# A graph network on one core: the count stretch's one-hot keys, four chunks in one two-tensor operation

## The chip, the core and the metric

The kernel runs on one core of one Trainium2 chip. The metric is device time in microseconds from the first to the last instruction of one execution, median of several runs; lower is better. The engines are named as in the profile: PE (matrix products) with PEld (its weight loads), DVE (the vector engine), ACT (the scalar engine), POOL (GpSimd, which here also issues the indirect gathers) and SP (which issues most other DMAs).

## What is computed

A stack of four graph networks over 3125 nodes with 128 features and 100,000 edges, sorted by destination, each with a residual connection. Cut to its core:

```python
edge_index = jnp.stack([src, dst])
h = jnp.maximum(_layernorm(x, axis=-1), 0.0)
x = x + _L0_gnn_ref(h, ...)   # 3 attention layers, softmax over each node's incoming edges
h = jnp.maximum(_layernorm(x, axis=-1), 0.0)
x = x + _L1_gnn_ref(h, ...)   # messages: an MLP on (h[src], h[dst], edge_attr), mean per node
h = jnp.maximum(_layernorm(x, axis=-1), 0.0)
x = x + _L2_gnn_ref(h, ...)   # 2 attention layers with 4 heads
h = jnp.maximum(_layernorm(x, axis=-1), 0.0)
x = x + _L3_gnn_ref(h, ...)   # 2 convolutions with normalized edge weights
```

In the first of these networks an edge's attention weight depends on its source and its destination node alone, so parallel edges weigh the same. What the kernel needs is therefore the number of edges from each node to each node:

```python
e = leaky_relu((h @ a_src[l])[src] + (h @ a_dst[l])[dst], 0.2)
p = exp(e - m[dst]);  s = segment_sum(p, dst);  alpha = p / s[dst]
z = segment_sum(alpha[:, None] * h[src], dst) + b[l]
```

## The kernel before

Nodes stand in NT = 25 tiles of P = 128. Edges are sorted by destination, so the edges of a small range of destinations are a run in memory. A *window* is NW = 16 destinations; there are 196. Its edges are loaded from a start that is found at run time, as k chunks of 128 edges (one edge per partition), with k fixed ahead from the distribution (`Plan`, `plan.cw`): edges that belong to a neighbour window are masked. An edge is packed in one integer `code`. The windows come in four batches, each decoded at once:

- batch 1, 8 windows of 59, 25, 20, 17, 15, 13, 12 and 12 chunks
- batch 2, 32 windows: 8 each of 11, 8, 7 and 6 chunks
- batch 3, 64 windows: 8 of 6, 24 of 5 and 32 of 4 chunks
- batch 4, 92 windows: 24 of 4 and 68 of 3 chunks

That is 1025 chunks in all. The stages follow each other: preparation and count (`count_edges`, up to 440 us), the three attention layers (to about 1070), the messages (to about 2190), the two attention layers with four heads (`dynamic_attention_layer`, to about 4560) and the two convolutions.

**The count stretch.** The count of edges from source node s to destination d is a product of one-hot matrices. For each chunk, `by_src` (128 edges x 128) marks the low seven bits of the edge's source, and `by_key` (128 edges x n_key = 400) marks its key, that is the source's tile (25) times 16 plus the destination's place in the window. PE multiplies `by_src` (the stationary operand) by `by_key` (the moving one) and adds the chunks of a window up in one PSUM bank; banks A, B and C take turns. Then ACT copies the bank to `count` as bytes (L1096), and runs a ReLU with a sum over it (L1099), which flags counts over 255. `by_src` is made for up to eight chunks by one two-tensor comparison in the helper `even` (L1040, recorded as L1043): the row of low bits is broadcast, the chunks are the innermost dimension, and an odd number of chunks is rounded up. `by_key` is made chunk by chunk by a comparison of the constant row `iota_key` with one number per partition (L1092), into six buffers.

Before each batch, `code` (one buffer) is loaded by one DMA per window on SP's queue (L1058), decoded by DVE (L1071 to L1080) and copied to `keep` by ACT (L1081); `keep` is stored (L1082) for later. The next batch's loads can start when `code` has been decoded. The tile framework reorders instructions on each engine, so the layer norm at the start (L866 to L877) and the decoding are interleaved with the products.

**The layers with four heads.** Edges come in 30 larger windows (`plan.ew`) of 59, 43, 30 ... 18 and 8 chunks, in groups of C = 4 chunks: 220 groups in a layer. For each group POOL issues four gathers into one buffer `g2` of a pool of G2 = 20 (`gather`, L1348), PE adds its transposes to the other term (L1376), DVE and ACT make the scores; a window later the group's message is made from the same buffer (L1847), which frees it, and summed by PE (L1852). The constant G2 also decides how far apart a window's scoring and its sums are issued: where the steps (groups) of windows i - 1, i and i + 1 add up to less than G2, the sums of window i - 1 are left for the next round (`apart`). For windows 15 to 20 these sums are 21, 20, 19, 18, 18 and 18.

Beside these layers the generator `adjacency` builds the weighted adjacency of the convolutions with one-hot products of its own (L1771, L1775), a step at a time; each of the 196 windows ends with a copy to `rows` on ACT (L1781; two buffers, as the pool has) and a store on SP's queue (L1782).

Of the kernel before, what the change touches and what calls it, by code (L numbers as in the profile page):

```python
# [8 lines left out]
F32 = mybir.dt.float32  # L9
BF16 = mybir.dt.bfloat16  # L10
I32 = mybir.dt.int32
AF = mybir.ActivationFunctionType
ALU = mybir.AluOpType
# [5 lines left out]
P = 128  # L19
C = 4  # L20
# [673 lines left out]
F16 = mybir.dt.float16  # L694
U8 = mybir.dt.uint8
SP = mybir.EngineType.SP
NW = 16
# [47 lines left out]
def sorted_path(ctx: ExitStack, tc: tile.TileContext, a: dict, out: bass.AP, flag_out: bass.AP):  # L745

    nc = tc.nc
# [21 lines left out]
    def bc(ap, shape):  # L769
        return ap.to_broadcast(shape)  # L770
# [32 lines left out]
                   allow_small_or_imprecise_dtypes=True)  # L803
    iota_by = const.tile([P, P, 8], BF16, name="iota_by")
    nc.vector.tensor_copy(iota_by, bc(iota_row[:, :, None], [P, P, 8]))
    weights = []

    def load_matrix(name, src):
# [231 lines left out]
    def even(out_t, a_t, row, j0, n, op):  # L1040

        n += n % 2
        nc.vector.tensor_tensor(out_t[:, :, :n], a_t[:, :, :n], bc(row[:, None, j0:j0 + n], [P, P, n]), op)  # L1043

    def count_edges(count):

        with tc.tile_pool(name="f_cw", bufs=2) as wp:
            tail0 = plan.nw * NW
            nc.vector.memset(count[:, :, tail0:], 0)
            many = wp.tile([P, plan.nw], F32, name="many", bufs=1)  # L1050
            below_255 = wp.tile([P, 1], F32, name="below_255", bufs=1)
            nc.vector.memset(below_255, -254.0)
            for w0, w1, c0, cols in plan.batches:
                code = wp.tile([P, cols, 2], I32, name="code", bufs=1)
                own = wp.tile([P, cols], F32, name="own", bufs=1)
                for w, col, k in plan.cw[w0:w1]:
                    r = at_register(base_c, w, P * k)
                    reads.append(nc.sync.dma_start(  # L1058
                        code[:, col - c0:col - c0 + k, :],
                        codes[bass.ds(r, P * k), :].rearrange("(p k) i -> p k i", p=P)))  # L1060
                    nc.gpsimd.memset(own[:, col - c0:col - c0 + k + k % 2], float(w))
                    if k % 2:
                        nc.gpsimd.memset(code[:, col - c0 + k:col - c0 + k + 1, :], 0)
                ti = wp.tile([P, cols], I32, name="ti", bufs=1)
                tf = wp.tile([P, cols], F32, name="tf", bufs=1)
                keep = wp.tile([P, 3, cols], F32, name="keep", bufs=2)
                key = keep[:, 0, :]
                low = wp.tile([P, cols], BF16, name="low", bufs=2)
                code_i = code[:, :, 0]

                nc.vector.tensor_scalar(ti, code_i, 16, None, ALU.logical_shift_right)  # L1071
                nc.vector.tensor_tensor(own, ti, own, ALU.not_equal)
                nc.vector.tensor_scalar(ti, code_i, 127, None, ALU.bitwise_and)
                nc.vector.scalar_tensor_tensor(keep[:, 1, :], own, FAR, ti, ALU.mult, ALU.add)
                nc.vector.tensor_copy(low, keep[:, 1, :])

                nc.vector.tensor_scalar(ti, code_i, 12, NW - 1, ALU.logical_shift_right, ALU.bitwise_and)
                nc.vector.tensor_copy(tf, ti)
                nc.vector.tensor_scalar(ti, code_i, 7, 31, ALU.logical_shift_right, ALU.bitwise_and)
                nc.vector.scalar_tensor_tensor(key, ti, float(NW), tf, ALU.mult, ALU.add)  # L1080
                nc.scalar.copy(keep[:, 2, :], code[:, :, 1].bitcast(F32))  # L1081
                nc.sync.dma_start(kept[:, :, c0:c0 + cols], keep)  # L1082
                for w, col, k in plan.cw[w0:w1]:
                    pt = bank("ABC"[w % 3])
                    for k0 in range(0, k, 8):
                        kn = min(8, k - k0)
                        j0 = col - c0 + k0
                        by_src = wp.tile([P, P, 8], BF16, name="by_src", bufs=3)
                        even(by_src, iota_by, low, j0, kn, ALU.is_equal)
                        for i in range(kn):  # L1090
                            by_key = wp.tile([P, n_key], BF16, name="by_key", bufs=6)
                            nc.vector.tensor_scalar(by_key, iota_key, key[:, j0 + i:j0 + i + 1], None,  # L1092
                                                    ALU.is_equal)
                            nc.tensor.matmul(pt[:, :n_key], by_src[:, :, i], by_key,  # L1094
                                             start=(k0 + i == 0), stop=(k0 + i == k - 1))
                    nc.scalar.copy(count[:, :, w * NW:(w + 1) * NW],  # L1096
                                   pt[:, :n_key].rearrange("p (t d) -> p t d", d=NW))
                    junk = wp.tile([P, n_key], BF16, name="junk")
                    nc.scalar.activation(junk, pt[:, :n_key], AF.Relu, bias=below_255,  # L1099
                                         accum_out=many[:, w:w + 1])  # L1100
            worst = wp.tile([P, 1], F32, name="worst", bufs=1)
            nc.vector.tensor_reduce(worst, many, AX.X, ALU.add)
            pt = bank("D")
            nc.tensor.matmul(pt[:1, :1], worst, ones[:, 0:1], start=True, stop=True)
            nc.vector.tensor_copy(flags[:, 3:4], pt[:1, :1])
            load_edge_windows(wp)
            for t in range(NT):
                own_t = count[:, t, t * P:(t + 1) * P]
                nc.vector.tensor_add(own_t, own_t, ident)
# [630 lines left out]
    def adjacency(pool):  # L1740
        for t in range(NT):
            ws = [c for c in plan.cw if c[0] // per == t]
            c0, cols = ws[0][1], ws[-1][1] + ws[-1][2] + ws[-1][2] % 2 - ws[0][1]
            pk = pool.tile([P, 3, cols], F32, name="pk", padded_shape=[P, 3, most_cols])
            nc.sync.dma_start(pk, kept[:, :, c0:c0 + cols])
            low = pool.tile([P, cols], BF16, name="low", padded_shape=[P, most_cols])
            w1 = pool.tile([P, cols], BF16, name="w1", padded_shape=[P, most_cols])
            w2 = pool.tile([P, cols], BF16, name="w2", padded_shape=[P, most_cols])
            w3 = pool.tile([P, cols], BF16, name="w3", padded_shape=[P, most_cols])
            yield  # L1750
            nc.scalar.copy(low, pk[:, 1, :])
            nc.scalar.copy(w1, pk[:, 2, :])
            nc.vector.tensor_sub(pk[:, 2, :], pk[:, 2, :], w1)
            nc.scalar.copy(w2, pk[:, 2, :])
            nc.vector.tensor_sub(pk[:, 2, :], pk[:, 2, :], w2)
            nc.scalar.copy(w3, pk[:, 2, :])
            yield
            for w, col, k in ws:
                sums = bank("W")
                for k0 in range(0, k, C):  # L1760
                    kn = min(C, k - k0)
                    j0 = col - c0 + k0
                    by_src = pool.tile([P, P, C], BF16, name="by_src")
                    even(by_src, iota_by, low, j0, kn, ALU.is_equal)
                    by_wgt = [pool.tile([P, P, C], BF16, name=f"by_wgt{q}") for q in range(3)]
                    for q, part in enumerate((w1, w2, w3)):
                        even(by_wgt[q], by_src, part, j0, kn, ALU.mult)
                    yield
                    by_key = pool.tile([P, C, n_key], BF16, name="by_key")
                    for i in reversed(range(kn)):  # L1770
                        nc.vector.tensor_scalar(by_key[:, i, :], iota_key, pk[:, 0, j0 + i:j0 + i + 1],  # L1771
                                                None, ALU.is_equal)
                    for i in range(kn):
                        for q in range(3):
                            nc.tensor.matmul(sums[:, :n_key], by_wgt[q][:, :, i], by_key[:, i, :],  # L1775
                                             start=(k0 + i + q == 0),
                                             stop=(k0 + i == k - 1 and q == 2))
                    if k0 + kn < k:
                        yield
                rows = pool.tile([P, n_key], F32, name="rows")  # L1780
                nc.scalar.copy(rows, sums[:, :n_key])  # L1781
                nc.sync.dma_start(adj[t, :, w % per, :], rows)  # L1782
                yield

    most_cols = max(sum(c[2] + c[2] % 2 for c in plan.cw if c[0] // per == t) for t in range(NT))

    G2 = 20


    def dynamic_attention_layer(i_layer, R3, T3, beside):  # L1790
# [230 lines left out]
```

## Time and profile before

| | us |
|---|---|
| median of 17 runs | 4943.17 (4925.3 to 4958.4) |
| the profiled execution, time | 4939.0 |
| its span | 4937.2 |
| PE / PEld busy | 4333.6 / 3613.5 |
| DVE busy | 3402.6 |
| POOL busy | 2659.4 |
| ACT busy | 1757.2 |

The profile is of one execution. Its views give, for each engine, busy time; for each group of instructions (line, engine, operation, tiles and shapes) the count, the busy time, the mean time of one and the idle time before it with what ended it; and the instructions in order of time, neighbours of one kind merged, as start, length, engine, line and count. A row's mean includes the part in which the next instruction on the engine has already begun, so the pace of a sequence is read from starts. The share of busy time differs from stage to stage:

| stage | us | PE | DVE | ACT | POOL |
|---|---|---|---|---|---|
| 0 to 92 | 92 | 13.8 | 47.4 | 7.5 | 21.5 |
| 92 to 440, count | 348 | 255.5 | 338.2 | 206.7 | 8.3 |
| 440 to 1070 | 630 | 534.0 | 508.8 | 483.2 | 8.4 |
| 1070 to 2190 | 1120 | 1025.7 | 530.4 | 376.1 | 812.9 |
| 2190 to 3390, first layer with heads | 1200 | 1114.7 | 945.9 | 290.5 | 898.9 |
| 3390 to 4560, second | 1170 | 1062.4 | 885.5 | 319.9 | 909.4 |
| 4560 to 4937 | 377 | 327.5 | 146.4 | 73.4 | 0 |

### The profile page before, as it was taken

The numbers are of one execution on the slowest core, as the hardware profiler recorded it, in microseconds if no ns is written. First come the engines' busy times: TensorE is split into PE (matmuls) and PEld (weight loads), VectorE is DVE, ScalarE is ACT, GpSimd is POOL, SyncE is SP. The second block draws the span as 40 slices with busy tenths as digits, with TensorE's granted clock in tenths as the row PEclk, the third lists the DMA queues.
The fourth block names the chain that finished last, engine by engine and source line by source line (L and its number), as shares of the span: only waits on it lengthen the run. The fifth ranks groups of instructions, "written<-read, shape, count | busy, mean of one in ns | idle before, by whom it ended". The sixth has DMA issues, their size and how long they took to land.

```text
span 4937.2 us, 85632 instructions
## 1 busy us (share of the span) xinstructions
PE 4333.6 (88%) x30361; PEld 3613.5 (73%) x30361; DVE 3402.6 (69%) x9835; ACT 1757.2 (36%) x4234; POOL 2659.4 (54%) x3155
## 2 busy tenths in 40 slices
PE   3777988969999999969999999997899999998898
PEld 1334988958788888857777777775778777777798
DVE  6999887864344545556887887875778787787433
ACT  0367877852233334331222222222222232222211
POOL 1000000037777777747777777774777777777000
PEclk9999999979999999979999999998999999999899
DMA  2010000033443434423333333332343333332575
GB/s 55 12 14 16 1 2 1 1 81 107 101 104 104 107 102 104 105 56 76 80 82 86 89 87 91 88 84 63 87 101 103 97 102 95 99 100 78 214 254 200
DMA packets 299196, 423.25 MB, mean 86 GB/s; under 512 B 113379, under 2 KB 243089, under 8 KB 292613
## 3 DMA queue, kind: packets, MB, share of 16 engines
q1 hardware_dynamic: 215589, 248.15, 17.2%
q0 software_dynamic: 80800, 166.13, 14.0%
q8 instruction: 241, 3.95, 0.3%
q10 hardware_dynamic: 2368, 3.40, 0.3%
q14 instruction: 198, 1.62, 0.1%
HBM read 367.97 MB, written 49.45 MB: 85 GB/s over the span
## 4 chain that ended last, share of the span: by engine, by line
PE 54%; DVE 13%; DMA 12%; POOL 10%; issue 7%; ACT 2%; SPq 2%; DVEq 0%; POOLq 0%; ACTq 0%
DMA g<-tab,src_i 11%; POOL g L1348 10%; PE W L1775 7%; PE A L1376 6%; PE C L1852 5%; PE sp L1813 4%; PE C L1925 4%; DVE by_key L1092 3%; PE A L1187 3%; PE B L1187 3%; PE A L1371 3%; PE B L1376 3%; PE C L1577 2%; PE C L1187 2%; PE D L1564 2%
## 5 line engine op out<-in xcount | busy, mean ns | idle before, releaser
L1348 POOL DMA_INDIRECT g<-tab,src_i x2520 | 2629.5, 1043 | 1696.9 <-ACT R L1326 827.1
L1364 DVE TENSOR_TENSOR w<-iota_row,dst_l 128x512 f32<-128x512 f32 (+2 forms) x660 | 435.5, 661 | 487.1 <-PE C L1577 459.6
L1376 PEld LDWEIGHTS A<-ident,g 128*128 128x128 f32 x3360 | 458.0, 202 | 267.8 <-DMA g<-tab,src_i 226.8
L1775 PE MATMUL W<-by_key,by_wgt 128*128 128x400 bf16 x3075 | 626.3, 351 | 7.0 <-DVE by_key L1771 6.1
L1376 PE MATMUL A<-ident,g 128*128 128x128 f32 x3360 | 491.3, 291 | 159.2 <-DMA g<-tab,src_i 158.2
L1806 ACT ACTIVATE low_y<-A 128x512 f32<-128x512 f32 (+3 forms) x440 | 254.2, 578 | 946.1 <-PE A L1376 938.1
L1852 PE MATMUL C<-msg,w 128*128 128x132 f32 x3360 | 486.3, 294 | 12.5 <-DVE msg L1847 4.4
L1775 PEld LDWEIGHTS <-by_wgt 128*128 128x128 bf16 x3075 | 355.5, 119 | 179.9 <-issue 48.4
L1807 DVE TENSOR_TENSOR low_y<-A,low_y 128x512 f32<-128x512 f32 (+3 forms) x440 | 291.2, 662 | 276.5 <-ACT low_y L1806 275.0
L1852 PEld LDWEIGHTS C<-msg,w 128*128 128x128 f32 x3360 | 432.6, 200 | 22.5 <-issue 7.2
L1813 PEld LDWEIGHTS sp<-att_h,low_y 128*128 128x128 f32 x3360 | 435.5, 202 | 10.4 <-DVE low_y L1807 8.7
L1813 PE MATMUL sp<-att_h,low_y 128*128 128x4 f32 x3360 | 424.8, 249 | 6.6 <-DVE low_y L1807 6.3
L1043 DVE TENSOR_TENSOR by_wgt<-by_src,w 128x512 bf16<-128x512 bf16 (+1 forms) x918 | 328.7, 397 | 63.4 <-PE W L1775 61.7
L1371 PE MATMUL A<-at,R 128*128 128x512 bf16 (+3 forms) x1320 | 361.1, 382 | 3.8 <-DVE at L1359 1.7
L1094 PEld LDWEIGHTS <-by_src 128*128 128x128 bf16 x1025 | 134.0, 149 | 274.0 <-DVE by_key L1092 158.8
L1636 ACT ACTIVATE x<-B,mb 128x512 f32<-128x512 f32 (+1 forms) x220 | 146.6, 667 | 428.3 <-PE B L1376 428.2
L1771 DVE TENSOR_SCALAR by_key<-iota_key,pk 128x400 bf16<-128x400 f16 x1025 | 295.5, 331 | 3.4 <-PE W L1775 3.1
L1847 DVE TENSOR_TENSOR msg<-g,ex 128x512 f32<-128x512 f32 (+3 forms) x440 | 286.9, 659 | 6.9 <-ACT ex L1831 6.4
L1376 PEld LDWEIGHTS B<-ident,g 128*128 128x128 f32 x1680 | 213.3, 192 | 106.7 <-DMA g<-tab,src_i 101.2
L1376 PE MATMUL B<-ident,g 128*128 128x128 f32 x1680 | 233.8, 281 | 64.8 <-DMA g<-tab,src_i 64.2
L1184 DVE TENSOR_TENSOR p<-p,count 128x1024 f32<-128x1024 f32 (+1 forms) x225 | 281.6, 1263 | 12.0 <-ACT p L1183 7.0
L1371 PEld LDWEIGHTS <-R 128*128 128x128 bf16 x1980 | 196.2, 102 | 125.8 <-issue 18.0
(404 smaller groups left out, 7519.9 us busy)
## 6 DMA issues: line engine op xcount, KB each, us to landing
A<-adj SPq DMA_DIRECT2D x48, 1600.0 KB
row<-place_d SPq DMA_DIRECT2D x597, 128.0 KB
g<-tab,src_i POOLq DMA_INDIRECT x2520
adj<-rows SPq DMA_DIRECT2D x196, 200.0 KB
er<-in_edge_attr_dram SPq DMA_DIRECT2D x39, 512.0 KB
tab<-T SPq DMA_DIRECT2D x21, 192.0 KB
row<-place_d SPq DMA_DIRECT2D x24, 96.0 KB
A<-adj SPq DMA_DIRECT2D x2, 800.0 KB
```

What stands on the lines that cost most here:

```text
L1043: nc.vector.tensor_tensor(out_t[:, :, :n], a_t[:, :, :n], bc(row[:, None, j0:j0 + n], [P, P, n]), op)
L1187: nc.tensor.matmul(acc, p[:, i * P:(i + 1) * P], T[:, st, :], start=(st == 0 and i % 3 == 0), stop=(st == NT - 1), skip_group_check=True)
L1348: nc.gpsimd.indirect_dma_start(out=g[:, j0 + c, :], out_offset=None, in_=tab, in_offset=bass.IndirectOffsetOnAxis(ap=src_i[:, c0 + c:c0 + ...
L1364: nc.vector.tensor_tensor(w[:, :n, :], bc(iota_row[:, None, :], [P, n, P]), bc(dst_l[:, c0:c0 + n, None], [P, n, P]), ALU.is_equal)
L1371: nc.tensor.matmul(pt[:, :n * P], R3[i][:, t * D:(t + 1) * D], at[:, :n * P], start=(i == 0), stop=False, skip_group_check=True)
L1376: nc.tensor.matmul(pt[:, c * P:(c + 1) * P], g[:, j0 + c, :], ident, start=False, stop=(c == n - 1), skip_group_check=True)
L1771: nc.vector.tensor_scalar(by_key[:, i, :], iota_key, pk[:, 0, j0 + i:j0 + i + 1], None, ALU.is_equal)
L1775: nc.tensor.matmul(sums[:, :n_key], by_wgt[q][:, :, i], by_key[:, i, :], start=(k0 + i + q == 0), stop=(k0 + i == k - 1 and q == 2))
L1807: nc.vector.tensor_max(low_y[:, :n * P], y1[:, :n * P], low_y[:, :n * P])
L1813: nc.tensor.matmul(sp[:, c * HEADS:(c + 1) * HEADS], low_y[:, c * P:(c + 1) * P], att_h, start=True, stop=True)
L1847: nc.vector.tensor_mul(msg[:, :n * HEADS, :HD], gs[j0 // C][:, :n, :].rearrange("p c (h d) -> p (c h) d", d=HD), bc(e[:, :, None], [P, n * ...
L1852: nc.tensor.matmul(acc[:, :AW], w[:, c, :], msg[:, c * HEADS:(c + 1) * HEADS, :].rearrange("p h d -> p (h d)"), start=(i == first_of[t] an ...
```

## The change

In the count stretch, `by_key` is made for up to four chunks by one two-tensor comparison through `even`, with the chunks innermost, as `by_src` is. For that there is a new constant `iota_kby`, the row of keys with each one repeated C = 4 times, and a copy `key16` of the decoded keys in 16 bits, made by ACT once per batch. PE reads its moving operand from every fourth element of the piece. `by_key` has three buffers of four chunks in place of six of one. To find room for the larger tiles, `rows` gets one buffer in place of two, and G2 is 19 in place of 20.

```diff
+    iota_kby = const.tile([P, NT * NW, C], F16, name="iota_kby")
+    nc.vector.tensor_copy(iota_kby, bc(iota_key[:, :, None], [P, NT * NW, C]))
...
     def even(out_t, a_t, row, j0, n, op):

         n += n % 2
-        nc.vector.tensor_tensor(out_t[:, :, :n], a_t[:, :, :n], bc(row[:, None, j0:j0 + n], [P, P, n]), op)
+        nc.vector.tensor_tensor(out_t[:, :, :n], a_t[:, :, :n],
+                                bc(row[:, None, j0:j0 + n], [P, a_t.shape[1], n]), op)
...
                 nc.vector.scalar_tensor_tensor(key, ti, float(NW), tf, ALU.mult, ALU.add)
+                key16 = wp.tile([P, cols], F16, name="key16", bufs=2)
+                nc.scalar.copy(key16, key)
...
-                        for i in range(kn):
-                            by_key = wp.tile([P, n_key], BF16, name="by_key", bufs=6)
-                            nc.vector.tensor_scalar(by_key, iota_key, key[:, j0 + i:j0 + i + 1], None,
-                                                    ALU.is_equal)
-                            nc.tensor.matmul(pt[:, :n_key], by_src[:, :, i], by_key,
-                                             start=(k0 + i == 0), stop=(k0 + i == k - 1))
+                        for i0 in range(0, kn, C):
+                            by_key = wp.tile([P, n_key, C], BF16, name="by_key", bufs=3)
+                            even(by_key, iota_kby, key16, j0 + i0, min(C, kn - i0), ALU.is_equal)
+                            for i in range(i0, min(i0 + C, kn)):
+                                nc.tensor.matmul(pt[:, :n_key], by_src[:, :, i], by_key[:, :, i - i0],
+                                                 start=(k0 + i == 0), stop=(k0 + i == k - 1))
...
-                rows = pool.tile([P, n_key], F32, name="rows")
+                rows = pool.tile([P, n_key], F32, name="rows", bufs=1)
                 nc.scalar.copy(rows, sums[:, :n_key])
                 nc.sync.dma_start(adj[t, :, w % per, :], rows)
...
-    G2 = 20
+    G2 = 19
```

In the order in which the changed kernel's instructions stand, the copy to `iota_kby` comes on DVE right after `ident_bf` (L793), and `key16` of batch 1 comes on ACT after the layer norm's square (L869). The rest of DVE's order is the same, with pieces in place of keys; in the layers with heads the order of PE, ACT and SP differs around window 17.

## The prediction

> **What bounds the kernel now.** I read the busy time by stage first, then the groups of the count stretch by form, then instructions in order of time there, then the gather queue of the two attention layers with four heads.
>
> The stage view has the stretch's length and count, then PE, PEld, DVE, ACT and POOL busy, the granted clock and the DMA share.
>
> ```profile
> 92.00:440.00 348.00, 255.49 (x999) 130.08 (x1000) 338.23 (x1258) 206.74 (x587) 8.30 (x248) 0.96 0.08 11
> ```
>
> DVE is busy 338 of 348 us of the count stretch, and nothing else is near it. Its groups (110 to 440 us, by form; last figures: busy us, mean ns, idle before):
>
> ```profile
> L1092 DVE TENSOR_SCALAR by_key<-iota_key,keep 128x400 bf16<-128x400 f16 x942 | 238.7, 315 | 0.1
> L1094 PEld LDWEIGHTS <-by_src 128*128 128x128 bf16 x941 | 121.6, 149 | 208.7 <-DVE by_key L1092 158.8 <-DVE by_src L1043 9.9 <-issue 5.0
> ...
> L1043 DVE TENSOR_TENSOR by_src<-iota_by,low 128x512 bf16<-128x512 bf16 x135 | 56.6, 419 | 0.0
> ...
> L1043 DVE TENSOR_TENSOR by_src<-iota_by,low 128x1024 bf16<-128x1024 bf16 x33 | 22.4, 678 | 0.0
> ```
>
> DVE never waits (0.1 us); PE waits for by_key. Means contain overlap with the next instruction, so I take start-to-start times, from the order of time, first where a window has eight chunks left, then where it has three:
>
> ```profile
> 96.25 0.68 DVE L1043 TENSOR_TENSOR by_src<-iota_by,low 128x1024 bf16<-128x1024 bf16 x1
> 96.86 1.95 DVE L1092 TENSOR_SCALAR by_key<-iota_key,keep 128x400 bf16<-128x400 f16 x8
> ...
> 98.72 0.68 DVE L1043 TENSOR_TENSOR by_src<-iota_by,low 128x1024 bf16<-128x1024 bf16 x1
> ```
>
> ```profile
> 438.04 0.43 DVE L1043 TENSOR_TENSOR by_src<-iota_by,low 128x512 bf16<-128x512 bf16 x1
> 438.38 0.80 DVE L1092 TENSOR_SCALAR by_key<-iota_key,keep 128x400 bf16<-128x400 f16 x3
> ...
> 439.08 0.43 DVE L1043 TENSOR_TENSOR by_src<-iota_by,low 128x512 bf16<-128x512 bf16 x1
> ```
>
> Eight keys take 1.86 us and three 0.70: 0.2335 us each. A two-tensor operation takes 0.601 us for 1024 elements (the trace's exact starts; 0.61 and 0.34 in these rounded lines), 0.333 for 512 and, from other rows, 0.468 for 768 and 0.201 for 256: two elements per 0.96 GHz cycle and 0.068 us fixed.
>
> **The change, part by part.** *The keys.* 1025 operations of 400 elements become 263 pieces of 1600 elements and 43 of 800, because a piece of three chunks is padded to four and one of a single chunk to two (`even`). By the two-tensor line a 1600 piece is 833 + 68 = 0.901 us and an 800 piece 0.417 + 0.068 = 0.485. Four single keys are 0.934, three are 0.700, one is 0.234. So a full piece gains 0.033 and a padded three loses 0.20. By batch of windows, pieces against keys:
> - batch 1: 43 x 0.901 + 3 x 0.485 = 40.2 against 173 x 0.2335 = 40.4: -0.2
> - batch 2: 64 and 8 pieces, 61.5 against 59.8: +1.7
> - batch 3: 64 and 32 pieces, 73.2 against 69.1: +4.1
> - batch 4 (68 of 92 windows have three chunks): 92 pieces, 82.9 against 70.1: +12.8
>
> Together +18.4. Bounds: at one element per cycle (the float32 two-tensor rows: 512 elements in 0.60) a piece is 1.73 and the four batches cost about +256; at the pace of the old key (four per cycle) it is 0.485, and what is left of that gain is about -50, since batch 3 would wait for its codes and a batch-4 window for ACT (count, ReLU and read-out start 1.04 us apart now). I take two per cycle: all four sizes of the same line, all operands 16 bits, lie on it, and the old key shows that f16 in, bf16 out does not lose the packing (0.234 is under the 0.276 that two per cycle would need).
>
> The row first: the old key needs 0.234 us for 400 elements. [...]
>
> *What batch 3 loses is hidden.* DVE's idle time in brackets:
>
> ```profile
> 324.36 1.01 DVE L1092 TENSOR_SCALAR by_key<-iota_key,keep 128x400 bf16<-128x400 f16 x4
> 334.90 0.35 DVE L1071 TENSOR_SCALAR ti<-code 128x368 int32<-128x368 int32 x1 [9.54 <-DMA code<-codes]
> ```
>
> Batch 4's 92 code loads leave SP's queue one by one from 230.0 to 333.4 us, once batch 3's decoding has freed `code`. That start moves with everything before it, its end as much, so 4.1 of batch 3 fits into 9.5 us of idle time. Without that cover it costs 4.1.
>
> *PE reads the keys at a pitch of four elements.* No row has a strided moving operand. Nearest are the weight loads, from the page:
>
> ```profile
> L1775 PEld LDWEIGHTS <-by_wgt 128*128 128x128 bf16 x3075 | 355.5, 119 | 179.9 <-issue 48.4
> ...
> L1371 PEld LDWEIGHTS <-R 128*128 128x128 bf16 x1980 | 196.2, 102 | 125.8 <-issue 18.0
> ```
>
> Pitch 1 is 102 ns, pitch 4 is 119, pitch 8 (L1094) is 149. A 400-column matmul starts every 0.167 us at full clock where PE is the limit (L1775). Scaled by 1.17 it is 0.195, by 1.46 0.244. DVE now gives one chunk every 0.300 us (eight: 0.601 + 1.802) to 0.41 (three), so nothing is lost between those bounds; the price begins at 0.300. I take 0.
>
> *The new copy of the keys.* `key16` is made on ACT, between DVE's `key` and the first piece. In batch 1 the built order puts it behind the layer norm's square:
>
> ```profile
> 69.65 2.89 ACT L869 ACTIVATE T<-Z 128x3200 f32<-128x3200 f32 x1 [10.72 <-DVE Z L868]
> ...
> 70.67 2.19 DVE L1092 TENSOR_SCALAR by_key<-iota_key,keep 128x400 bf16<-128x400 f16 x9
> ...
> 72.78 3.48 DVE L870 TENSOR_REDUCE ln_st<-T 128x25 f32<-128x3200 f32 x1
> ```
>
> The nine keys that filled DVE's wait for the square can't start: +2.1 (0 to 3). In the other batches DVE waits for a copy like L1081's (0.35 to 0.53 us) and two hand-offs, with the previous window's count already done on ACT: 0.6 each, batch 3's hidden as above: +1.2 (0 to 3). `iota_kby` stands before the chain to `found`, `base` and the first codes; `iota_by` took 0.60 us for 1024, so 1600 are +0.9 (0.4 to 1.7).
>
> *G2 from 20 to 19* removes a gather buffer. Gathers follow each other every 1.25 us (median) and wait for no buffer today. Group 19 of a layer would now wait for the message product of group 0:
>
> ```profile
> 2292.23 0.95 POOL L1348 DMA_INDIRECT g<-tab,src_i  x1 [0.30 <-issue]
> ```
>
> ```profile
> 2294.88 1.29 DVE L1847 TENSOR_TENSOR msg<-g,ex 128x512 f32<-128x512 f32 x2
> ```
>
> The first product ends at 2295.57: 3.3 us late in layer 0, and 1.4 in layer 1 (3491.21 against 3492.59). All other groups keep over 1 us. Behind the waiting gather stands the whole gather queue, and PE waits for gathers for 158 us: +4.7 (0, if PE's backlog covers it, to 6). The same constant decides `apart`; only window 17 (steps 7 + 6 + 6 = 19) changes sides, so the sums of window 16 are issued one window earlier. The work is the same: 0 (-10 to +10).
>
> *One `rows` buffer.* ACT's next copy waits until the last one has landed. Rows are 12 us apart on average, at the closest:
>
> ```profile
> 4012.04 0.49 ACT L1781 COPY rows<-W 128x400 f32<-128x400 f32 x1 [2.39 <-PE W L1775]
> ...
> 4015.19 0.49 ACT L1781 COPY rows<-W 128x400 f32<-128x400 f32 x1
> ```
>
> [...] ACT's next low_y and PE's next W product stand behind them; the gather queue covers most: +2 (0 to 10).
>
> **Sum.** -0.2 + 1.7 + 12.8 (keys) + 2.1 + 1.2 + 0.9 + 4.7 + 2.0 = +25.2. The profiled run took 4939.0 us (span 4937.2), so 4964 there; it lies 4.2 below the median of the runs, 4943.2, which gives 4968.
>
> **The rivals.**
> - *The layers give it back* (not slower). From window 17 on, where the order changes, the gathers take 359 us in each layer where 256 at 1.25 us would be 319: 80 us lost in two layers to gathers of 1.6 to 4.6 us. If the moved sums thin these out by more than 25 us of the 80, the time is at or under 4943; with 30, 4938. For it: DVE and POOL are both busy there. Against: the same DVE work runs in the same stretch. 0.10.
> - *PE becomes the bound.* If a strided column costs twice, a chunk is 0.333 us and the windows with eight chunks go by PE: +14, 4982. At 0.400 it is +64, 5032. For it: the weight loads lengthen with the pitch. Against: their ratio is far from 2. 0.07.
> - *The pieces run at one element per cycle*: +256 - 9.5 hidden + 10.9 for the rest: about 5200. Against: line L1043. 0.03.
> - *It does next to nothing*: the later stages absorb it, as batch 3 does; within 4933 to 4953. Against: attention, messages and layers follow the count in series. 0.08.
>
> **How the numbers follow.** The main case has 0.72, own range 4954 to 4984: the copies and G2 at their low ends, rows and order at their high ends. To leave out no more than 2 in 10 I take 4945 to 4995: the whole main case, the first price of the second rival and the upper part of the last. A measurement tells 0.2%, about 10 us, from no change. Slower: 0.70 of the main case's 0.72, 0.07, 0.03 and 0.02 of the last: 0.82. Faster: half of the first rival, 0.05. Same: 0.13.
>
> **What would show it.** Right: pieces start 0.90 us apart and windows of three chunks take 1.23 us (1.035 before); the idle time before batch 4's first decode falls from 9.5 to about 5; the count stretch ends 17 to 19 us later; group 19's gather waits 3.3 and 1.4 us; PE keeps waiting for by_key. Wrong: DVE idle before pieces because PE holds their buffers, pieces of 0.48 or 1.73 us, or layers whose length from first to last gather (1155 and 1165 us) moves by over 10.

## The result: 5004 us, and the profile after

The changed kernel took 5004.18 us (median of 6 runs, 4993.78 to 5013.1), the kernel before 4941.53 (35 runs): ratio 1.0124, 95% interval 1.0107 to 1.0141, or 62.6 us longer. The direction was as forecast, the size was not: 5004 lies above the range of 4945 to 4995. The profiled execution has a span of 5004.9 us.

Line numbers move by a few: `even` is recorded at L1045, the count's matmul is L1099, the gather L1353, the message L1852, `rows` L1786. The stage view of the changed kernel (stretch, its length, then busy us and count of PE, PEld, DVE, ACT, POOL, granted clock, DMA share, GB/s):

```profile
92.00:440.00 348.00, 330.21 (x899) 126.69 (x898) 323.18 (x492) 175.09 (x488) 7.86 (x248) 0.97 0.08 11
```

DVE was the one full engine of this stretch, 338 of 348 us against PE's 255. Now PE is ahead: 330 us, with about 100 matmuls fewer done by 440 us. The groups by form (110 to 482 us) say who waits for whom:

```profile
L1045 DVE TENSOR_TENSOR by_key<-iota_kby,key 128x1600 bf16<-128x1600 f16 x243 | 238.3, 984 | 10.3 <-PE A L1099 2.9 <-PE C L1099 2.8 <-PE B L1099 2.3
...
L1099 PE MATMUL C<-by_key,by_src 128*128 128x400 bf16 x321 | 128.0, 544 | 10.0 <-DVE by_key L1045 9.8 <-ACT junk L1104 0.2
```

and the same row of the kernel before (110 to 440 us):

```profile
L1094 PE MATMUL C<-by_key,by_src 128*128 128x400 bf16 x321 | 83.3, 354 | 40.6 <-DVE by_key L1092 40.6
```

The last figures of a row are the idle time before the group and what ended it. DVE, which did not wait for PE before a key (0.1 us idle in all), waits for PE to give a piece's buffer back, and a matmul has a mean of 544 ns, where it was 354 before. In order of time PE is one unbroken run in a window of eight-chunk groups, while in a window of three chunks DVE still paces:

```profile
93.61 9.92 PE L1099 MATMUL A<-by_key,by_src 128*128 128x400 bf16 x27
```

```profile
478.86 0.97 DVE L1045 TENSOR_TENSOR by_key<-iota_kby,key 128x1600 bf16<-128x1600 f16 x1
...
479.76 0.41 DVE L1045 TENSOR_TENSOR by_src<-iota_by,low 128x512 bf16<-128x512 bf16 x1
...
480.10 0.97 DVE L1045 TENSOR_TENSOR by_key<-iota_kby,key 128x1600 bf16<-128x1600 f16 x1
```

27 matmuls in 9.92 us are about 0.36 us each (the last one's length left out); before, a chunk came every 0.31 (eight in 2.47). A three-chunk window takes 1.24 us, as the prediction had it (1.23), against 3 x 0.36 = 1.08 on PE.

Where the 67.7 us between the two profiled spans arise (start or end of the same instruction in both traces):

| mark | before | after | difference |
|---|---|---|---|
| first count matmul | 71.05 | 75.74 | +4.7 |
| last count matmul, end | 440.59 | 482.40 | +41.8 |
| first message gather | 1059.15 | 1102.34 | +43.2 |
| first gather, layer 0 with heads | 2194.78 | 2239.04 | +44.3 |
| last gather, layer 0 | 3349.33 | 3410.77 | +61.4 |
| last gather, layer 1 | 4558.47 | 4623.12 | +64.7 |
| end | 4937.22 | 5004.93 | +67.7 |

So there are two losses: some 42 us in the count stretch, where 18.5 were forecast, and some 20 in the layers with heads, where 6.7 were.

### The profile page after: what moved, and what is told of

It reads as the page before. It is cut to its first block, busy times and chain, and to the rows that moved or that the text cites. A ratio compares the mean times of both kernels' runs of the same rounds, so it can differ in the third digit from the quotient of the medians.

```text
span 5004.9 us, 85164 instructions
## 1 busy us (share of the span) xinstructions
PE 4475.2 (89%) x30361; PEld 3640.8 (73%) x30361; DVE 3426.3 (68%) x9117; ACT 1761.7 (35%) x4238; POOL 2670.8 (53%) x3155
## 5 line engine op out<-in xcount | busy, mean ns | idle before, releaser
L1353 POOL DMA_INDIRECT g<-tab,src_i x2520 | 2641.4, 1048 | 1730.6 <-ACT R L1331 851.2
L1045 DVE TENSOR_TENSOR by_wgt<-by_src,w 128x512 bf16<-128x512 bf16 (+1 forms) x918 | 328.5, 397 | 65.0 <-PE W L1780 64.1
L1099 PEld LDWEIGHTS <-by_src 128*128 128x128 bf16 x1025 | 142.4, 148 | 312.2 <-issue 202.0
L1381 PE MATMUL B<-ident,g 128*128 128x128 f32 x1680 | 235.0, 282 | 63.2 <-DMA g<-tab,src_i 62.6
L1045 DVE TENSOR_TENSOR by_key<-iota_kby,key 128x1600 bf16<-128x1600 f16 (+1 forms) x306 | 280.4, 926 | 15.5 <-PE A L1099 5.0
```

The costliest lines, as they stand in the source:

```text
L1353: nc.gpsimd.indirect_dma_start(out=g[:, j0 + c, :], out_offset=None, in_=tab, in_offset=bass.IndirectOffsetOnAxis(ap=src_i[:, c0 + c:c0 + ...
L1381: nc.tensor.matmul(pt[:, c * P:(c + 1) * P], g[:, j0 + c, :], ident, start=False, stop=(c == n - 1), skip_group_check=True)
```

## The experiments

My theory for the first loss: PE reads its moving operand at a pitch of 4 elements (8 bytes), and that takes more than twice as long, so PE becomes the bound. The rival: pieces, their three buffers and their hand-over cost the time, whatever PE reads. For the second: the missing gather buffer, against the moved order at window 17, the single `rows` buffer, and plain variation between runs.

One thing is needed to read the numbers. The runs of experiments 1, 4 and 5 fell on other chips (three, one for each experiment), on which the kernel before takes 6244 to 6253 us. The count stretch is the same there: with the keys of before its last matmul ends at 439.5 to 441.5 us in four profiles, and at 438.9 to 440.6 in three where the kernel before takes 4942. From the messages on the time is longer: from their first gather to the last one of the layers 4777 us in dense_old (1080.9 to 5858.0), 3498 in before (1059.2 to 4557.5). Times of the count stretch are therefore compared across chips, each of one profiled execution and good to a us or two; whole times only with the kernel before on the same chip.

### 1. The same pieces, read at other pitches

```diff
-    nc.tensor.matmul(pt[:, :n_key], by_src[:, :, i], by_key[:, :, i - i0], ...)
+    flat = by_key.rearrange("p k c -> p (k c)"); c = i - i0
+    read = <below> if kn - i0 > 2 else by_key[:, :, c]
+    nc.tensor.matmul(pt[:, :n_key], by_src[:, :, i], read, ...)
     # dense_read    flat[:, c * n_key:(c + 1) * n_key]
     # pitch2_read   flat[:, c % 2:2 * n_key:2]
     # pitch3_read   flat[:, c % 3:3 * n_key:3]
# pitch8: by_key [P, n_key, 8], of which [:, :, :4] is written and read;
#         by_key and by_src two buffers, key16 one
```

> The changed kernel, but the matmul of every piece of three or four chunks reads 400 neighbouring elements of the piece instead of every fourth one. Pieces, buffers, waits and order are as in the changed kernel; the counts are no longer the edge counts. Theory A (the strided read makes PE the bound): matmuls can again start every 0.17 to 0.2 us, PE's mean duration falls from 541 to about 350 ns, DVE sets the pace again, and the last count matmul, at 482.4 us in the changed kernel and 440.6 before, comes at 455 to 462; the whole is 4970 to 4985 us (before 4942, changed 5004). Rival B (three piece buffers and DVE's handing over of pieces set the pace, whatever PE reads): the last count matmul stays within 5 us of 482, the whole within 8 of 5004. Rival C (the pieces themselves slow DVE): as B, with pieces further apart than 0.90 us and PE waiting for them.

> The changed kernel, but the matmul of every piece of three or four chunks reads every second element of the piece's first 800; the counts are no longer the edge counts. If the price grows with the pitch in a straight line from 0.167 us per chunk at pitch 1 to 0.36 at pitch 4, matmuls that wait for nothing start every 0.23 us, DVE still sets the pace (0.30), and the last count matmul comes within 6 us of that of the kernel that reads neighbours. If any pitch over 1 costs twice, they start every 0.33 to 0.36 us and the last count matmul comes at about 482.

> The changed kernel, but the matmul of every piece of three or four chunks reads every third element of the piece's first 1200; the counts are no longer the edge counts. A price in a straight line with the pitch: matmuls that wait for nothing start every 0.30 us, and the last count matmul comes at 458 to 470. A step at pitch 2: 0.33 to 0.36 us, and about 482. A step between 2 and 4: this run tells on which side 3 lies.

> The changed kernel with pieces of eight elements per key, of which four are written and read: each matmul reads every eighth element (16 bytes). To make room there are two buffers for by_key and by_src and one for key16. If the price grows with the pitch: 0.55 to 0.75 us per chunk within a piece, and the count stretch ends 150 to 300 us after that of the changed kernel. If every strided read costs the same: 0.36 us within a piece, and the last count matmul comes at 482 to 500, the surplus from the fewer buffers.

Measured. Starts of successive matmuls are medians over those at full granted clock; for pitch 8 the clock was 0.5 nearly throughout.

| kernel | pitch | start to start, us | last count matmul, us |
|---|---|---|---|
| dense_read | 1 | 0.170 | 460.7 |
| pitch2_read | 2 | 0.183 | 460.1 |
| pitch3_read | 3 | 0.271 | 461.2 |
| changed kernel | 4 | 0.361 | 482.4 |
| pitch8 | 8 | 0.711 | 839.1 |

The stage view of dense_read, and PE in order of time there, at pitch 2 and at pitch 3, all in the first window:

```profile
92.00:440.00 348.00, 233.17 (x950) 125.21 (x949) 337.97 (x526) 191.92 (x541) 7.86 (x248) 0.92 0.08 11
```

```profile
97.42 1.74 PE L1102 MATMUL A<-by_key,by_src 128*128 128x400 bf16 x8 [0.67 <-DVE by_key L1045]
...
99.82 1.74 PE L1102 MATMUL A<-by_key,by_src 128*128 128x400 bf16 x8 [0.67 <-DVE by_key L1045]
```

```profile
96.33 1.78 PE L1102 MATMUL A<-by_key,by_src 128*128 128x400 bf16 x8 [0.62 <-DVE by_key L1045]
```

```profile
93.80 9.38 PE L1102 MATMUL A<-by_key,by_src 128*128 128x400 bf16 x32
```

With neighbouring elements DVE is the full engine again (338 of 348 us), PE does eight matmuls and then waits 0.67 us for a piece, and the pieces come every 2.40 us per eight chunks. Only what PE reads was changed, and 21.7 us are gone: theory A holds, and the rivals, which had the count stretch stay at 482, fall. (The whole took 6310.36 us there, 1.0118 of the kernel before, 1.0079 to 1.0157; with the layers as before it is experiment 4's dense_old, at 1.0020, so most of that is the layers' edits on that kind of chip.) At pitch 3 PE's 0.271 almost fills the 0.30 that DVE leaves it (32 matmuls in 9.38 us, 0.293 each); at pitch 4 its 0.361 is over it.

My straight line from pitch 1 to pitch 4 was wrong in form. From pitch 2 on each further element of pitch costs some 0.09 us per 400 columns; pitch 1 and 2 are 0.013 us apart. Worked out from the table: 400 x 2 bytes x pitch over the time is 8.7, 8.9, 8.9 and 9.0 bytes per ns and partition at pitches 2, 3, 4 and 8. So at these four pitches the time goes with the stretch that PE steps over; pitch 1 would be 0.09 us at that pace and takes 0.170. (Only 16-bit elements were measured, so whether bytes or elements count is not shown.) At pitch 4 the time does not follow the granted clock: in the changed kernel 39 starts at a granted clock of 0.5 have a median of 0.360 us, against 0.361 at full clock, while at pitch 1, in dense_read, 93 such starts have 0.333 against 0.170.

At pitch 8 the stage view and the order of time read:

```profile
92.00:838.00 746.00, 722.00 (x1013) 145.39 (x1012) 393.03 (x568) 213.15 (x591) 7.92 (x248) 0.50 0.04 5
```

```profile
99.70 8.71 PE L1099 MATMUL A<-by_key,by_src 128*128 128x400 bf16 x12
99.92 0.99 DVE L1045 TENSOR_TENSOR by_key<-iota_kby,key 128x1600 bf16<-128x1600 f16 x1 [1.58 <-PE A L1099]
```

Now every window goes by PE (1013 matmuls x 0.711 = 720 of the 746 us), DVE waits for PE before 133 pieces, 185 us in all, and the piece itself takes what it took (a mean of 989 ns, 984 in the changed kernel). I had 150 to 300 us more than the changed kernel; it is 357, since I had let the three-chunk windows go by DVE.

### 2. The keys of the change with the layers as before, and the layers' edits alone

```diff
# old_layers: the changed kernel with
-    G2 = 19
+    G2 = 20
-    rows = pool.tile([P, n_key], F32, name="rows", bufs=1)
+    rows = pool.tile([P, n_key], F32, name="rows")
     # iota_kby moves from the constants into the count stretch's pool
# before_g19: the kernel before, G2 = 19;  before_rows1: the kernel before, rows with bufs=1
```

> The changed kernel's keys with the layers as before: G2 is 20, rows has two buffers, and iota_kby lies in the count stretch's own pool. Theory A (the layers lose some 20 us to the missing gather buffer): the layers are as long as before, 1154 and 1165 us from first to last gather within 5, and the whole is 4980 to 4988 us. Rival (what the layers lost in the one profile is variation between runs, or comes from the later start): the whole is 4995 to 5005, and the ratio to the changed kernel's 5004 is within 0.2%. On record I had 4.7 us for G2 and 2 for rows: 4997.

> The kernel before with G2 at 19 alone. My sum on record: +4.7 us (0 to 6), no effect of the moved order, so 4942 to 4948. If the missing buffer cost the layers the 20 us that the profile of the changed kernel shows: 4958 to 4965.

> The kernel before with one rows buffer alone. My sum on record: +2 us (0 to 10). The profile of the changed kernel shows one wait of 0.3 us for a row to land, so now I expect 0: 4937 to 4946 us, with the layers' lengths as before within 5.

Measured, beside 4942.80 of the kernel before (23 runs): old_layers 4986.72, ratio 1.0090 (1.0074 to 1.0107), last count matmul at 482.0; before_g19 4953.20, 1.0026 (1.0013 to 1.0038), that is 6 to 19 us; before_rows1 4945.67, 1.0006 (0.9993 to 1.0018).

With the layers as before the whole loss is 43.9 us (37 to 53) and the count stretch's is 41.4: by the medians, what is lost in the count goes through to the end. A single profile can't show it: the profiled execution of old_layers, the fastest of its runs, ends 28.5 us after that of before, as its two layers with heads, with the code of before, are 5 and 9 us shorter. G2 and `rows` alone are 10.4 and 2.9, the latter not told from nothing; 43.9 + 10.4 + 2.9 = 57 of the 62.6, which the intervals cover. So the layers' share is mainly G2, and part of the 20 us in the one profile is variation: in the profile of before_rows1, whose median moves by 2.9, layer 0 is 5 us longer and the end 7 us later, and in that of before_g19 the two layers together are as long as before (1159 + 1161 against 1155 + 1165).

The gather queue in before_g19, layer 0, where group 19 begins:

```profile
2291.92 1.00 POOL L1348 DMA_INDIRECT g<-tab,src_i  x1 [0.30 <-issue]
2296.45 0.94 POOL L1348 DMA_INDIRECT g<-tab,src_i  x1 [3.52 <-PE A L1376]
```

and in the changed kernel:

```profile
2333.70 0.94 POOL L1353 DMA_INDIRECT g<-tab,src_i  x1 [0.30 <-issue]
2342.40 0.94 POOL L1353 DMA_INDIRECT g<-tab,src_i  x1 [7.75 <-PE A L1381]
```

Above the usual step of 1.25 us the gather is late by 3.3 us (2.1 in layer 1) in the one and 7.4 (0.9) in the other. The bracket names a PE instruction, but what frees the buffer is the message product of group 0, which ends 0.75 us before the gather in both; in the changed kernel it is the first of these two:

```profile
2340.98 1.28 DVE L1852 TENSOR_TENSOR msg<-g,ex 128x512 f32<-128x512 f32 x2
```

No other group waited for a buffer in these two profiles. A wait of this kind is not bound to 19 buffers, though: in before_rows1 and in half (experiment 3), which have 20, the gather of group 20 in layer 0 was late by 1.9 and 1.7 us, again starting 0.74 us after the product of group 0.

`rows` in the changed kernel, the group and one row of what ended its idle time:

```profile
L1786 ACT COPY rows<-W x196: 467/492/493, 2354.1 to 4574.2; 128x400 f32<-128x400 f32 x196
...
  DMA adj<-rows: 0.3, 1
```

Of 196 copies one waited for a store, 0.3 us.

### 3. Pieces for the first four chunks of a group only

```diff
 # old_layers, and in it
-    by_key = wp.tile([P, n_key, C], BF16, name="by_key", bufs=3)
-    even(by_key, iota_kby, key16, j0 + i0, min(C, kn - i0), ALU.is_equal)
+    # i0 == 0: a piece as above, in two buffers
+    # i0 == 4: keys one by one by tensor_scalar, as before, in four buffers
```

> Keys of the first four chunks of each group of eight in a piece, the others one by one as before; layers as before (G2 20, two rows buffers). PE needs (4 x 0.36 + 4 x 0.167) = 2.1 us per eight chunks and DVE 2.4, so DVE sets the pace in groups of eight, and in groups of up to four PE's 0.36 us stands against DVE's 0.37 to 0.41. Theory A: last count matmul 3 to 20 us after the 440.6 of before, the whole 4940 to 4962 us. If the loss is in pieces as such (waits and buffers): half of it stays or more, the last count matmul at 460 or later.

Measured: 4966.16 us, ratio 1.0048 (1.0035 to 1.0061), last count matmul at 462.1. In the count stretch I expected 3 to 20 us and got 21.6; the whole is 23.4 us longer, above the 4940 to 4962 expected. The groups by form:

```profile
L1106 PE MATMUL A<-piece,by_src 128*128 128x400 bf16 x255 | 104.8, 541 | 1.2 <-DVE piece L1043 0.7
...
L1106 PE MATMUL C<-by_key,by_src 128*128 128x400 bf16 x63 | 16.4, 359 | 0.0
```

The kernel is not half of each: most windows have fewer than eight chunks, and 805 of 1025 chunks stayed in pieces. By what I had put down, a last matmul at 460 or later spoke for the rival; with so few single keys the run can't tell the two apart, and dense_read is what decides. What it does show is the two kinds of matmul side by side: 541 ns read at pitch 4, 359 read at pitch 1.

### 4. The buffer or the order; no strided read; a layout that PE can read

```diff
# buf19_order20: the kernel before, 19 gather buffers, order by 20
-    G2 = 20
+    G2 = 19
-    apart = steps(i - 1) + steps(i) + steps(i + 1) < G2 if i else False
+    apart = steps(i - 1) + steps(i) + steps(i + 1) < 20 if i else False
# buf20_order19: G2 = 20, order by 19.   dense_old: old_layers with dense_read's edit
# pairs: the kernel before, and for a full four chunks in batches 2 to 4 (iota_kby [P, n_key, 2], on ACT)
+    pairs = wp.tile([P, 2, n_key, 2], BF16, name="pairs", bufs=3)
+    nc.vector.tensor_tensor(pairs, <iota_kby, both pairs>, <key16, pair and chunk>, ALU.is_equal)
+    read = pairs[:, i // 2, :, i % 2]      # all other keys one by one, in three buffers
```

> The kernel before with 19 gather buffers, the order of the sums decided with 20 as before. Before with both at 19 came to 1.0026 [1.0013, 1.0038]. Theory A (the buffer's wait, on record 4.7 us; the gather of group 19 waited 3.3 and 2.1 us there) : +3 to +8 us, ratio 1.0006 to 1.0016. Theory B (all of it is the moved order at window 17): ratio 1.000 +- 0.001.

> The kernel before with 20 gather buffers and the order of the sums decided with 19: the sums of window 16 are issued one window earlier. On record I took 0 for it (-10 to +10). Theory A: ratio 1.000 +- 0.001. Theory B: +6 to +13 us, ratio 1.0013 to 1.0026.

> Pieces only where a full four chunks are left and only in batches 2 to 4 (136 pieces), laid out as two pairs: element order pair, key, chunk in the pair, so PE reads every second element; all other keys one by one as before; G2 20, two rows buffers; the repeated iota is made on ACT. If a piece of four still takes 0.90 us on DVE: 136 x (0.934 - 0.90) = 4.6 us saved, less some 2 us of waits for key16, so the last count matmul at 436 to 441 (440.6 before) and the whole 4936 to 4944 us, the same as before within 0.2%. If DVE runs at one element per cycle with two elements innermost: pieces 1.73 us, +113 us in the count stretch less what batch 4's wait hides.

> The changed kernel's pieces, with PE reading 400 neighbouring elements of each piece of three or four chunks (the counts are no longer the edge counts), and the layers as before (G2 20, two rows buffers, iota_kby in the count stretch's pool). With the strided read and the same layers it was 1.0090 [1.0074, 1.0107], last count matmul at 482.0. Theory A (the strided read is some 21 of those 42 us, the pieces themselves 20): last count matmul at 459 to 462, ratio 1.003 to 1.005. Rival (something else in the pieces): 475 or later, ratio 1.007 or more.

Measured, against 6244.40 us of the kernel before: buf19_order20 1.0068 (1.0041 to 1.0094), buf20_order19 1.0033 (1.0005 to 1.0061), pairs 0.9975 (0.9951 to 0.9999), dense_old 1.0020 (0.9994 to 1.0047) with the last count matmul at 461.2. The last agrees with dense_read in the count stretch: 482.0 - 461.2 = 20.8 us for the strided read. The pieces of pairs, in order of time:

```profile
154.38 1.89 DVE L1100 TENSOR_TENSOR pairs<-iota_kby,key 128x1600 bf16<-128x1600 f16 x2
...
155.42 1.79 PE L1112 MATMUL C<-pairs,by_src 128*128 128x400 bf16 x8 [0.75 <-DVE pairs L1100]
```

136 pieces start 0.902 us apart, as with four chunks innermost, and PE reads them at pitch 2 as fast as at pitch 2 above (eight in 1.79 us). So both layouts do 1600 elements in 0.902 us, where the line of `by_src`'s rows has 0.901. The count stretch ends at 439.3 us, and at 440.0 in the repetition, where seven profiles with single keys have 438.9 to 441.5: the repaired piece gains nothing that can be told from the spread.

### 5. Again

> The kernel before with 19 gather buffers and the order of the sums decided with 20, to be read where the kernel before takes about 4942 us (where it takes 6244 it measured 1.0068 [1.0041, 1.0094]). Theory A (the buffer's waits are what G2 costs): +5 to +12 us, ratio 1.001 to 1.0025. Theory B (the moved order): 1.000 +- 0.001. On record: +4.7 us.

> The kernel before with 20 gather buffers and the order decided with 19 (1.0033 [1.0005, 1.0061] where the kernel before takes 6244 us). Theory A: 1.000 +- 0.001. Theory B: +6 to +13 us, 1.0013 to 1.0026. On record: 0 (-10 to +10).

> The changed kernel's pieces, PE reading neighbouring elements (the counts are no longer the edge counts), layers as before. Where the kernel before takes 4942 us: if the 20.6 us by which its last count matmul is later goes through to the end, 4960 to 4965, ratio 1.0037 to 1.0047. If later stages absorb it: under 1.003. With the strided read the same layers took 4986.7.

> Pieces of two pairs where four full chunks are left, in batches 2 to 4; the rest as in the kernel before. Its last count matmul came at 439.3 us against 440.6, so 4936 to 4946 us, ratio 0.999 to 1.001, where the kernel before takes 4942. A real gain of the 0.25% that it showed where that takes 6244 us would be 4930.

The kernel before took 6252.85 us, so the question of the usual speed stays open. Measured: b19_again 1.0058 (1.0029 to 1.0087), o19_again 1.0008 (0.9980 to 1.0036), dense_old_again 1.0025 (1.0004 to 1.0045), pairs_again 1.0007 (0.9979 to 1.0035). The buffer is confirmed twice, the order is not (one interval is above 1, the other holds it). Its size can't be carried over: on these chips gathers wait for a buffer some 100 times in the two layers, with 19 buffers (550 + 489 us in buf19_order20) and with 20 (about 519 + 509 in buf20_order19), against twice in before_g19. The pieces with neighbouring elements cost 12 and 16 us by the ratios of dense_old and its repetition; that agrees with the 20 us of the count stretch, but the intervals are too wide to say how much of it arrives at the end. For pairs the two results together show no difference from the kernel before, and no version here beats it.

## Why the prediction was off, point by point

**The step that failed** is "PE reads the keys at a pitch of four elements", where I took 0. I scaled 0.167 us (the shortest start to start of L1775 at full clock; the median is 0.169) by how weight loads lengthen with the pitch (1.17 to 1.46) and got 0.195 to 0.244, under the 0.300 at which, as I wrote, the price begins. It measured 0.361. The weight loads were a poor stand-in: from pitch 4 to 8 they lengthen by 30 ns for 128 columns (119 to 149), the matmul by 350 ns for 400 (361 to 711), nearly four times as much per column. What sets them apart was not looked into. The strided read cost 21 to 22 us in the count stretch (482.4 - 460.7 and 482.0 - 461.2).

**The rival "PE becomes the bound"** was the right mechanism with its price bracketed: +14 at 0.333, +64 at 0.400. Worked out in the same way with 0.36 the four batches cost 50.6 in place of 18.4; less the 5.4 us that are left of batch 4's wait for codes, it is 27 more than my sum, 4995; the 9 us that are missing then are no more than G2 and the intervals leave open. By batch that way has 8.4, 9.7, 9.0 and 4.9 us. From dense_read to the changed kernel the end of batch 1 moves by 8.1, that of batch 2 by 9.1 more, the start of batch 4 by 0.7 less, and the end by 5.2 more: as worked out, but that nothing of batch 3's share is left at the start of batch 4. I gave this rival 0.07 and my range let it in only up to its first price. The other three rivals did not come: the layers gave nothing back and later stages absorbed nothing that the medians show, and a piece takes 0.90 us.

**The pieces on DVE** were right: 0.90 us apart, 1.24 us for three-chunk windows. The prediction's cycle is, in the profile of before, the 1.04 ns by which one more float32 element lengthens a two-tensor row (L1847, means of 285 ns at 128 elements and 683 at 512); two per cycle are the 1.92 elements per ns between `by_src`'s 0.201 us at 256 and 0.601 at 1024, and four per cycle the 3.8 of the 16-bit tensor-scalar rows (L1359, 255 ns at 128 and 357 at 512). Without the strided read the count ends 20.1 to 20.8 us late, against 18.5 in my sum. That this is so near is in part luck, as the marks by batch show:

| matmul | before | dense_read | changed | forecast without the read |
|---|---|---|---|---|
| first of batch 1, start | 71.1 | 75.2 | 75.7 | |
| last of the first window, end | 102.7 | 102.6 | 105.7 | |
| last of batch 1, end | 138.6 | 138.8 | 146.9 | +2.8 |
| last of batch 2, end | 224.1 | 227.3 | 244.5 | +5.1 |
| first of batch 4, start | 340.2 | 348.0 | 364.5 | +5.7 |
| last of batch 4, end | 440.6 | 460.7 | 482.4 | +18.5 |

Batch 4 itself loses 12.4 us, as forecast (12.8). Before it two errors of opposite sign partly cancel: batch 1 loses 0.2 in place of 2.8, and between the ends of batch 2 and the start of batch 4 it is 4.5 in place of 0.6.

**The cover by batch 4's codes** came as forecast on DVE, idle time of about 5 us before its first decode: without the strided read it is 4.7 (the bracket below says issue, but ACT's copy of the same codes waited for their DMA until then). In the changed kernel DVE comes there late and the wait is gone. What the cover gave, 4.9 us, the copy behind it took back (next point).

**The copies `key16`** were wrong in both places. In batch 1 the first matmul is 3.9 to 4.8 us later in all kernels with that copy there, against 3.0 for it and `iota_kby`, but by the end of the first window nothing of it is left in dense_read; where it was made up was not traced. In batch 4 I had 0.6. First the kernel before, then dense_read, from the decode (334.90 and 337.31) to the first key:

```profile
339.84 2.18 DVE L1092 TENSOR_SCALAR by_key<-iota_key,keep 128x400 bf16<-128x400 f16 x9
```

```profile
337.31 0.35 DVE L1074 TENSOR_SCALAR ti<-code 128x368 int32<-128x368 int32 x1 [4.68 <-issue]
...
345.97 0.29 DVE L1117 TENSOR_TENSOR count<-count,ident 128x128 uint8<-128x128 uint8 x1 [1.90 <-ACT count L1104]
346.94 2.80 DVE L1045 TENSOR_TENSOR by_key<-iota_kby,key 128x1600 bf16<-128x1600 f16 x3 [0.68 <-ACT key L1085]
```

4.9 us became 9.6: DVE waits for PE and ACT to finish the windows before, and then for the copy. That is 4.7, mostly work queued ahead of the copy rather than the copy: ACT, which had stood waiting for the codes too, reads out nine windows, 0.95 us each, between its copy of the codes and `key16`. I had the previous window's count as already done.

**G2** was mis-sized in its sum: the waits I read off were right in before_g19 (3.3 and 2.1 us against 3.3 and 1.4), but the time is 6 to 19 us longer, not 4.7. That the rest is the moved order is not shown. The changed kernel's own profile has 7.4 and 0.9.

**`rows`**: no run shows the +2 of the sum. What they showed is one wait for a store in each profile with one buffer, 0.3 us in the changed kernel and 0.5 in before_rows1, and a time that can't be told from that of the kernel before (1.0006).

## What to carry to other kernels

A batched operation that puts the batch innermost makes its reader read with a stride; price that reader too, here, from pitch 2 to 8 of 16-bit elements, from the stretch spanned and not from elements read, and keep the pitch where the reader is still nearly as fast as with neighbouring elements (here two 16-bit elements for PE, 0.183 us against 0.170). When the cheap engine has a margin of under two on the bound one (0.170 us of PE against 0.300 of DVE per chunk), a doubled price of an access (0.361) is enough to make it the bound. A size that must shrink to make room (a buffer ring) is an edit of its own, to be timed alone.

## What the hardware showed that was not expected

PE's price of a strided moving operand, in 16 bits, goes by the stretch spanned, 8.7 to 9.0 bytes per ns and partition from 4 bytes of pitch on; at 8 bytes it is the same at full and at half granted clock (0.361 and 0.360 us). At pitch 8, in one profile, PE is busy 722 of 746 us and the granted clock is 0.50 in them, while the pitch-4 kernel, nearly as busy (330 of 348), had 0.97.

On the chips where the kernel before takes 6244 to 6253 us, engines stand in the layers for tens of microseconds in "issue", a wait for nothing that the profile shows. From the view of waits of o19_again, 2505 to 2680 us (total, times, longest):

```profile
POOL g L1348 <- PE sp L1813: 70.3, 1, 70.3
...
ACT low_y L1806 <- issue: 43.1, 2, 35.5
```

In the profile of before the gather of that place (group 20 of layer 0) did not wait for a buffer, and in before_rows1 it was late by 1.9 us. The mean granted clock of the kernel before is 0.84 to 0.85 on those chips and 0.93 to 0.94 where it takes 4942 us; whether that is a cause or follows from PE's waits was not shown. What holds the queues up there was not found.
